# The last block's second product in an AdaLN and mixture-of-adapters kernel: five of seven products on two levels, two seeded in PSUM, and the bias as a row of the adapters' weights

## The chip, the cores and the metric

One core of one Trainium2 chip. The metric is the device time of one execution in microseconds. The kernel before has a median of 261.63 us over 3 runs (261.48 to 261.75).

## What is computed

All in fp32, for 64 batches of 64 tokens with 512 features:

```python
q = relu(cond @ W3 + b3)                          # 64 x 512, one row for each batch
v = relu(((64 * x + x.sum(1)) * q) @ W2 + b2)     # first product, 512 x 512
base = v @ W_base + b_base                        # second product, 512 x 512
gates = softmax(v @ W_router + b_router)          # 6 experts, the two largest are kept
h = v @ [A_s, A_r]                                # 7 adapters of rank 16: 112 columns
out = x + base + (h * [1, kept gates]) @ [B_s; B_r]
```

## The kernel before, in words

The tokens are cut into four blocks (k = 0 to 3), each of two halves h of 512 tokens; features lie on the partitions, in four chunks of 128. A block goes through a first product (W2), the adapters' and router's product `ph` (8 groups of 128 tokens), the gate, and a second product (W_base).

Both products use a scheme of seven block products in place of eight: features in two halves, tokens in two halves, with row sums `s` or `sy` (`row_sums`, L255) and weight sums `t2`, `tb` (`weight_sums`, L130). In blocks 1 to 3 the first product applies the scheme a second time within each of the seven (`first_inner`, L424, "two levels"): an inner product is one matmul of 128 x 128 weights with 256 columns (`q`, L443), and seven of them stand for eight. Their inner row sums come from `prepare_inner` (L299), partly on GpSimd (L333), their inner weight sums from `inner_weight_sums` (L144). An inner step has two PSUM banks: `a` holds products 1 and 2 in its low half, 5 and 3 in its high half; `b` holds 6 in the low half, 7 and 4 in the high half. ScalarE copies the low half of `a` to that of `b` (`seed_y`), and that to `b`'s high half (`seed_z`); VectorE or ScalarE take the results out (`take_...`).

The second product (`second`, L616) has one level in all blocks: `prod(i, j, name)` is two matmuls of 512 columns into a bank, `seed` a ScalarE copy from bank to bank, `with_x` (L634) a VectorE step that adds the bank, the bias column `bb_sb` and the rows of x, and `routed` (L640) the adapters' part. `gate` (L574) runs on VectorE with one exponential on ScalarE; the weighting into `hw` (L683) follows; eight transposes (`pt`, L704) turn it; ScalarE copies it to `hwT` (L706), and GpSimd forms the difference `hwd` (L708). In the last block the last two output rows are cut in 384 and 128 columns (L726), with the last output issued from ScalarE's queue.

The order on every engine is the order in which the program is written (`manual_schedule`). The fillers (`behind`, `fill`, `share`) hand out the preparation of block k + 1 during block k, and are empty in the last block. PSUM has six banks that rotate under one tag (`ps_p`) and a tile of two banks (`ps_h`) that `ph` and `pt` use in turn. Loads of x for the residual (`load_rows`, L606) and outputs go through the SP queue, which issues in order.

The last block's tail, as written before (L740 to L752):

```python
        prod(3, 0, "w", start=False)
        routed("w", 0, KH, hwd[:GR])
        leave(ps["w", 0], KH, 0, u12[0])
        ...
        for p, cols, queue in last:
            part(p, cols, 3, False)
            last_routed(p, cols, hwd)
            leave(p, KH + 1, 0, u12[1], cols, queue)
```

Of the kernel before, what the change touches and what calls it, by code (L numbers as in the profile page):

```python
# [32 lines left out]
HC = GR + E  # L33


@with_exitstack
def adaln_ffn(ctx: ExitStack, tc: tile.TileContext, xa, x0, x1, head, w3, w2, wb, a, bcat, br, outT):
# [25 lines left out]
    def load_x(k):  # L63
        xs[k] = xpool.tile([P, NC, 2, TB], F32, tag="x", name=f"x_{k}")
        for c in CHUNKS:
            nc.sync.dma_start(xs[k][:, c].rearrange("p h t -> p (h t)"), x1[k, c])
# [5 lines left out]
    def loaded(src, shape, name):  # L72
        t = const.tile(shape, F32, tag=name, name=name)
        nc.sync.dma_start(t, src)
        return t
# [9 lines left out]
    NH0 = NQ * B + 3 * NC  # L85
    head_sb = const.tile([P, NH0 + NQ * P], F32, tag="head_sb", name="head_sb")
    cond_sb = head_sb[:, : NQ * B].rearrange("p (c b) -> p c b", c=NQ)
    b3_sb, b2_sb, bb_sb = (head_sb[:, NQ * B + n * NC : NQ * B + (n + 1) * NC] for n in range(3))
# [30 lines left out]
    bcat_sb = loaded(bcat, [GR, D], "bcat_sb")  # L119
    load_x(1)  # L120

# [22 lines left out]
    def inner_weight_sums(w, t, name):  # L144

        at = {i: n for n, i in enumerate((5, 6, 7, 4, 1, 2, 3))}
        it = const.tile([P, 4, 7, P], F32, tag=name, name=name)

        def side(o, n):
            b = {1: t[o][:, 0, :P], 2: t[o][:, 1, :P], 3: t[o][:, 1, P:]}  # L150
            return b[n] if n in b else it[:, {5: 0, 6: 1, 7: 2, 4: 3}[n], at[o]]

        low = w.rearrange("p (o k) m -> p o k m", k=KH)
        groups = ((slice(0, 4), lambda c, m: t["sums"][:, :, c, ts(m, P)]),
                  (slice(4, 6), lambda c, m: low[:, :, c, ts(m, P)]),
                  (slice(6, 7), lambda c, m: t[3][:, c, ts(m, P)].unsqueeze(1)))
        steps = []
        for o, b in groups:
            i = [it[:, n, o] for n in range(4)]
            steps += [  # L160
                lambda i=i, b=b: nc.vector.tensor_tensor(i[0], b(0, 1), b(0, 0), ALU.subtract),
                lambda i=i, b=b: nc.vector.tensor_tensor(i[1], b(1, 1), i[0], ALU.subtract),
                lambda i=i, b=b: nc.vector.tensor_tensor(i[2], b(1, 1), b(0, 1), ALU.subtract),
                lambda i=i, b=b: nc.vector.tensor_tensor(i[3], b(1, 0), i[1], ALU.subtract),
            ]
        return side, steps
# [88 lines left out]
    def row_sums(a, name, cols=slice(0, TB)):  # L255

        all_s = mid.tile([P, 4, KH, TB], F32, tag=name, name=name)
        s = [all_s[:, i, :, cols] for i in range(4)]
        a11, a12, a21, a22 = a[:, :KH, 0, cols], a[:, KH:, 0, cols], a[:, :KH, 1, cols], a[:, KH:, 1, cols]

        def steps(c=slice(0, KH)):
            return [
                lambda: nc.vector.tensor_tensor(s[0][:, c], a21[:, c], a22[:, c], ALU.add),
                lambda: nc.vector.tensor_tensor(s[1][:, c], s[0][:, c], a11[:, c], ALU.subtract),
                lambda: nc.vector.tensor_tensor(s[2][:, c], a11[:, c], a21[:, c], ALU.subtract),
                lambda: nc.vector.tensor_tensor(s[3][:, c], a12[:, c], s[1][:, c], ALU.subtract),
            ]

        return {1: a11, 2: a12, 3: s[3], 4: a22, 5: s[0], 6: s[1], 7: s[2], "sums": all_s}, steps
# [3 lines left out]
    def fill(n):  # L273
        for _ in range(min(n, len(behind))):
            for step in behind.pop(0):
                step()
# [21 lines left out]

    def prepare_inner(k):  # L299
# [13 lines left out]
        def steps(g, a, engine=nc.vector):  # L313
            return [
                lambda: engine.tensor_tensor(s[g][:, 0], a(0, 1), a(1, 1), ALU.add),
                lambda: engine.tensor_tensor(s[g][:, 1], s[g][:, 0], a(0, 0), ALU.subtract),
                lambda: engine.tensor_tensor(s[g][:, 2], a(0, 0), a(0, 1), ALU.subtract),
                lambda: engine.tensor_tensor(s[g][:, 3], a(1, 0), s[g][:, 1], ALU.subtract),
            ]

# [103 lines left out]
    def first_inner(k, y):  # L424
# [94 lines left out]
        for step in inner[k]["late"]:  # L519
            step()  # L520
        fill(2)
# [52 lines left out]
    def gate(k, ph):  # L574
# [10 lines left out]
        nc.scalar.activation(g, lg, AF.Exp)  # L585
        sm = small.tile([P, 2 * NS], F32, tag="sm", name=f"sm_{k}")
# [11 lines left out]
        nc.vector.tensor_tensor(eq, gj, ge, ALU.is_equal)  # L598
        nc.vector.tensor_tensor(gt, gj, ge, ALU.is_gt)
        nc.vector.tensor_tensor(eq, eq, tri.unsqueeze(1).to_broadcast(pair), ALU.mult)  # L600
        nc.vector.tensor_tensor(gt, gt, eq, ALU.add)
        rank = small.tile(shape, F32, tag="rank", name=f"rank_{k}")
# [13 lines left out]
    def second(k, y, ph, res):  # L616
# [17 lines left out]
        def with_x(name, j, f, h):  # L634

            t = row(f, h)
            nc.vector.scalar_tensor_tensor(t, ps[name, j], bb_sb[:, f : f + 1], t, ALU.add, ALU.add)  # L637
            return t
# [9 lines left out]
        def part(p, cols, i, start):  # L648
            for c in range(KH):
                nc.tensor.matmul(  # L650
                    p[:, cols], tb[i][:, c, ts(1, P)], sy[i][:, c, cols], start=start and c == 0, stop=False,
                    skip_group_check=True,
                )

        def last_routed(p, cols, hw):
            nc.tensor.matmul(
                p[:, cols], bcat_sb[:, ts(KH + 1, P)], hw[:GR, cols], start=False, stop=True,
                skip_group_check=True,
            )

        def leave(p, f, h, add, cols=slice(0, TB), queue=nc.sync):
            nc.vector.tensor_tensor(add[:, cols], p[:, cols], add[:, cols], ALU.add)
            queue.dma_start(outT[k, f, h, :, cols], add[:, cols])
# [5 lines left out]
        def share():  # L669
# [12 lines left out]
        hw = small.tile([P, 2 * NS, GR], F32, tag="hw", name=f"hw_{k}")  # L682
        nc.vector.tensor_tensor(  # L683
            hw.rearrange("p s (g r) -> p s g r", r=R),
            ph[:, :, :GR].rearrange("p s (g r) -> p s g r", r=R),
            w.unsqueeze(3).to_broadcast([P, 2 * NS, G, R]),
            ALU.mult,
        )
# [12 lines left out]
        pt = ps_h.tile([P, 2 * NS, P], F32, tag="ph", name=f"pt_{k}")  # L701
        hwT = small.tile([P, 2, TB], F32, tag="hwT", name=f"hwT_{k}")
        for s in range(2 * NS):
            nc.tensor.transpose(pt[:GR, s, :], hw[:, s, :], ident)  # L704
        for h in range(2):
            nc.scalar.copy(hwT[:GR, h], pt[:GR, ts(h, NS)].rearrange("p s t -> p (s t)"))  # L706
        hwd = small.tile([P, TB], F32, tag="hwd", name=f"hwd_{k}")
        nc.gpsimd.tensor_tensor(hwd[:GR], hwT[:GR, 0], hwT[:GR, 1], ALU.subtract)  # L708
# [4 lines left out]
        routed("x", 0, 0, hwT[:GR, 0])  # L713
        finish("x", 0, 0, 0)
        routed("z", 0, 0, hwT[:GR, 1])
        finish("z", 0, 0, 1)

        routed("w", 0, KH, hwT[:GR, 1])
        leave(ps["w", 0], KH, 1, u22[0])
        share()  # L720
        if k < NB - 1:
            prod(5, 1, "w")
            routed("w", 1, KH + 1, hwT[:GR, 1])
            leave(ps["w", 1], KH + 1, 1, u22[1])
        else:
            last = [(ps_p.tile([P, TB], F32, tag="pp", name=f"last_{lo}"), slice(lo, hi), queue)  # L726
                    for lo, hi, queue in ((0, 3 * P, nc.sync), (3 * P, TB, nc.scalar))]
            for p, cols, queue in last:
                part(p, cols, 5, True)
                last_routed(p, cols, hwT[:, 1])  # L730
                leave(p, KH + 1, 1, u22[1], cols, queue)
        share()
        routed("x", 1, 1, hwT[:GR, 0])
# [3 lines left out]
        routed("z", 1, 1, hwT[:GR, 1])  # L737
# [3 lines left out]
        routed("w", 0, KH, hwd[:GR])  # L741
        leave(ps["w", 0], KH, 0, u12[0])
        share()
        if k < NB - 1:
            prod(3, 1, "w", start=False)
            routed("w", 1, KH + 1, hwd[:GR])
            leave(ps["w", 1], KH + 1, 0, u12[1])
            return
        for p, cols, queue in last:
            part(p, cols, 3, False)  # L750
            last_routed(p, cols, hwd)
            leave(p, KH + 1, 0, u12[1], cols, queue)  # L752
# [4 lines left out]
    inner_t, inner_steps = inner_weight_sums(w2_sb, t2, "inner_t")  # L757
    for k in range(NB):
# [14 lines left out]
        if not rest:  # L773
            groups.sort(key=lambda g: g[1] // KH)
        for n, (h, s) in enumerate(groups):
            if rest and n == 2:
                rest()
            for c in range(NC):
                nc.tensor.matmul(  # L779
                    ph[:, h * NS + s, :HC], y[:, c, h, ts(s, P)], a_sb[:, c, :],  # L780
                    start=(c == 0), stop=(c == NC - 1),
                )
        sys_[k], steps = row_sums(y, "sy")
# [54 lines left out]
```

## Time and profile before

| | |
|---|---|
| median of the runs | 261.63 us |
| the profiled execution: time | 261.56 us |
| its span in the trace | 259.8 us |
| last `ph` matmul ends, last block | 224.69 us |
| last matmul ends | 256.56 us |
| TensorE / VectorE / ScalarE / GpSimd busy | 254.8 / 193.9 / 136.5 / 38.7 us |
| copy of a bank of 512 columns on ScalarE (L629) | 571 to 573 ns |
| two-input add on VectorE, 256 / 512 / 1024 columns | 418 / 688 / 1219 ns |
| two-input add on GpSimd, 256 / 512 columns | 727 / 1270 ns |
| one output of 256 KB, issue to landing | 2.0 us |

The span runs from the first to the last event of the trace; the time of the execution has 1.76 us around it. In a row of the timeline the columns are the start, the duration, the engine, the line, the operation with output and inputs, and in brackets how long the engine sat idle before and what it waited for. In the chain the columns are start, duration, and what. PE is TensorE, PEld its weight loads, DVE VectorE, ACT ScalarE, POOL GpSimd, SPq and ACTq the DMA issues of those queues.

### The profile page before, as it was taken

How to read it: one execution, taken by the hardware profiler on the slowest of the kernel's cores; microseconds unless marked ns; L12 is line 12 of the kernel's file. 1: busy time of each engine (PE TensorE's matmuls, PEld its weight loads, DVE VectorE, ACT ScalarE, POOL GpSimd, SP SyncE). 2: the span in 40 equal slices, each digit the busy share in tenths (PEclk: the TensorE clock that was granted, in tenths of full speed). 3: DMA queues.
4: the chain of work that ended last, by engine and by line, in shares of the span. 5: the costliest groups of instructions: out<-in, count | busy, mean ns of one | idle time of the engine just before them, and what ended most of it. 6: DMA issues, size and time to landing. Idle time of an engine off the chain costs nothing.

```text
span 259.8 us, 3177 instructions
## 1 busy us (share of the span) xinstructions
PE 254.8 (98%) x1004; PEld 164.5 (63%) x1004; DVE 193.9 (75%) x386; ACT 136.5 (53%) x373; POOL 38.7 (15%) x53
## 2 busy tenths in 40 slices
PE   7999999999999999999999999999999999999995
PEld 3756896454478888444458889544447889745453
DVE  2899898799968967968995894988895475872332
ACT  2399496596048896289017889349404428112000
POOL 1000000020017610002006630002001770000100
PEclk9999999999999999999999999999999999999999
DMA  6997629303320044000521025200332023400233
GB/s 194 360 352 295 261 99 390 156 3 121 121 81 0 11 156 161 0 3 6 196 81 42 0 83 168 76 0 3 121 121 81 0 77 92 159 0 3 76 139 108
DMA packets 14145, 28.54 MB, mean 110 GB/s; under 512 B 1472, under 2 KB 2496, under 8 KB 14128
## 3 DMA queue, kind: packets, MB, share of 16 engines
q1 hardware_dynamic: 13840, 28.21, 30.6%
q8 instruction: 8, 0.13, 0.2%
q10 hardware_dynamic: 288, 0.13, 0.2%
q14 instruction: 9, 0.07, 0.1%
HBM read 19.94 MB, written 8.39 MB: 109 GB/s over the span
## 4 chain that ended last, share of the span: by engine, by line
PE 94%; ACT 2%; DMA 2%; SPq 0%; issue 0%; DVE 0%
PE ia L446 13%; PE ph L779 11%; PE oz L170 11%; PE ox L170 11%; PE ib L446 10%; PE ow L170 9%; PE py L354 5%; PE oy L170 5%; PE ow L641 5%; PE oz L641 3%; PE ox L641 3%; DMA w_sb<-in_w_dram 2%; PE yw L170 1%; PE pt L704 1%; PE last L650 1%; PE yz L170 1%
## 5 line engine op out<-in xcount | busy, mean ns | idle before, releaser
L212 ACT ACTIVATE x<-x,vsum,nq 128x64 f32<-128x64 f32 x192 | 67.5, 431 | 7.0 <-DVE vsum L208 7.0
L779 PE MATMUL ph<-a_sb,y 128*128 128x118 f32 x256 | 30.5, 276 | 0.3 <-ACT y L340 0.3
L779 PEld LDWEIGHTS ph<-a_sb,y 128*128 128x128 f32 x256 | 30.0, 192 | 1.2 <-ACT y L340 0.7
L437 DVE TENSOR_TENSOR u<-ib,u 128x256 f32<-128x256 f32 x42 | 16.4, 419 | 18.5 <-PE ib L446 18.3
L452 ACT COPY ib<-ia 128x256 f32<-128x256 f32 x21 | 7.6, 361 | 42.3 <-PE ia L446 42.3
L170 PE MATMUL ox<-y,wb_sb 128*128 128x512 f32 x64 | 29.5, 593 | 0.0
L708 POOL TENSOR_TENSOR hwd<-hwT 112x512 f32<-112x512 f32 x4 | 5.8, 1452 | 136.1 <-ACT hwT L706 136.1
L170 PEld LDWEIGHTS ox<-y,wb_sb 128*128 128x128 f32 x64 | 11.9, 190 | 13.4 <-issue 13.2
L437 DVE TENSOR_TENSOR u<-ia,u 128x256 f32<-128x256 f32 (+1 forms) x36 | 16.1, 462 | 2.9 <-ACT u L484 1.6
L446 PE MATMUL ib<-inner_s,inner_t 128*128 128x256 f32 x60 | 17.8, 384 | 0.0
L340 ACT ACTIVATE y<-u,head_sb 128x256 f32<-128x256 f32 (+1 forms) x30 | 15.8, 585 | 3.8 <-DVE u L412 3.2
L637 DVE SCALAR_TENSOR_TENSOR xu<-oz,head_sb,xu 128x512 f32<-128x512 f32 x16 | 12.0, 749 | 7.3 <-PE oz L170 4.8
L207 DVE TENSOR_REDUCE vsum<-x 128x8 f32<-128x512 f32 x24 | 16.2, 676 | 0.0
L170 PE MATMUL oz<-sy,tb 128*128 128x512 f32 x32 | 15.2, 599 | 0.0
L170 PE MATMUL oz<-y,tb 128*128 128x512 f32 x32 | 15.1, 593 | 0.0
L170 PE MATMUL oy<-sy,tb 128*128 128x512 f32 x32 | 15.0, 592 | 0.0
L354 PE MATMUL py<-v,w_sb 128*128 128x512 f32 (+1 forms) x40 | 14.4, 510 | 0.7 <-DMA w_sb<-in_w_dram 0.7
L170 PE MATMUL ow<-sy,tb 128*128 128x512 f32 x28 | 13.2, 592 | 0.0
L170 PE MATMUL ow<-sy,wb_sb 128*128 128x512 f32 x28 | 13.2, 592 | 0.0
L455 ACT COPY ib<-ib 128x256 f32<-128x256 f32 x21 | 7.6, 363 | 10.0 <-PE ib L446 10.0
L446 PEld LDWEIGHTS ib<-inner_s,inner_t 128*128 128x128 f32 x60 | 11.2, 190 | 2.2 <-ACT ib L455 0.8
L250 ACT ACTIVATE v<-x,vsum,nq 128x64 f32<-128x64 f32 x32 | 11.0, 427 | 1.7 <-DVE vsum L248 1.7
(173 smaller groups left out, 461.6 us busy)
## 6 DMA issues: line engine op xcount, KB each, us to landing
xu<-in_x_dram SPq DMA_DIRECT2D x16, 512.0 KB, 4.2
out_dram<-xu SPq DMA_DIRECT2D x30, 256.0 KB, 2.0
x<-in_x_dram SPq DMA_DIRECT2D x12, 512.0 KB, 7.5
x<-in_x_dram SPq DMA_DIRECT2D x7, 256.0 KB, 5.7
w_sb<-in_w_dram SPq DMA_DIRECT2D x4, 256.0 KB, 5.5
wb_sb<-in_wb_dram SPq DMA_DIRECT2D x4, 256.0 KB, 4.9
w_sb<-in_w_dram SPq DMA_DIRECT2D x1, 384.0 KB, 4.7
out_dram<-xu SPq DMA_DIRECT2D x2, 192.0 KB, 1.9
```

The lines of the kernel that those rows point to most:

```text
L170: nc.tensor.matmul(ps, w[i][:, c, ts(j, P)], s[i][:, c, :], start=start and c == 0, stop=c == KH - 1, skip_group_check=True,)
L207: nc.vector.tensor_reduce(vsum[:, c, bs], xc, AX.XY, ALU.add)
L212: nc.scalar.activation(x, x, AF.Identity, bias=vsum[:, c, b : b + 1], scale=nq[:, c, b : b + 1])
L250: nc.scalar.activation(v[:, c, :, ts(b, NH)], batches_of(c, b, b + 1)[:, :, 0], AF.Identity, bias=vsum[:, c, b : b + 1], scale=nq[:, c, b ...
L340: nc.scalar.activation(y[:, f, h, cols], src, AF.Relu, bias=b2_sb[:, f : f + 1])
L354: nc.tensor.matmul(p[:, :, lo * NH : hi * NH], w2_sb[:, c, ts(f, P)], v[:, c, :, lo * NH : hi * NH], start=(c == 0 and lo == 0), stop=(c = ...
L437: add = lambda o, a, b: nc.vector.tensor_tensor(o, a, b, ALU.add)
L446: nc.tensor.matmul(bank[b, t][:, cols], t_side(o, n), s_side(o, n), start=n == 1, stop=True, skip_group_check=True,)
L452: nc.scalar.copy(bank["b", t][:, lo], bank["a", t][:, lo])
L637: nc.vector.scalar_tensor_tensor(t, ps[name, j], bb_sb[:, f : f + 1], t, ALU.add, ALU.add)
L641: nc.tensor.matmul(ps[name, j], bcat_sb[:, ts(f, P)], hw, start=False, stop=True, skip_group_check=True)
L779: nc.tensor.matmul(ph[:, h * NS + s, :HC], y[:, c, h, ts(s, P)], a_sb[:, c, :], start=(c == 0), stop=(c == NC - 1),)
```

## The change

For blocks 0 to 2 `second` stays, with the bias no longer added by `with_x` but carried as row 113 of `bcat_sb`, against a column of ones in `hw`. In the last block `second` is replaced by `second_inner`: products 1, 2, 5, 4 and 3 on two levels (steps t = 0 to 4), products 6 and 7 on one level, each in a bank that ScalarE first fills with the partial sum it is to be added to. Three of its inner products stand between the groups of `ph`. GpSimd forms the inner weight sums in block 2, and in the last block most of the inner row sums, one of the outer ones, and two sums of outputs. The diff, cut to its core:

```diff
-            nc.vector.scalar_tensor_tensor(t, ps[name, j], bb_sb[:, f : f + 1], t, ALU.add, ALU.add)
+            nc.vector.tensor_tensor(t, ps[name, j], t, ALU.add)
...
+    bcat_sb = const.tile([GB, D], F32, tag="bcat_sb", name="bcat_sb")
+    nc.sync.dma_start(bcat_sb[:GR], bcat)
     load_x(1)
+    nc.sync.dma_start(bcat_sb[GR:], bb)
...
+        if k == NB - 2:   # first_inner, after the late sums; steps[4:] follow after hwd
+            wide["t"], wide["steps"] = inner_weight_sums(wb_sb, tb, ..., (5, 4), nc.gpsimd)
+            for step in wide["steps"][:4]:
+                step()
...
+    def gate(k, ph, between=()):   # others() after the exponential, after eq, and ahead of rank
...
+        order = (1, 2, 5, 4, 3)
+        place = {1: (0, (0, 1, 2, 3)), 2: (1, (0, 1, 2, 3)), 5: (1, (3, 1, 2, 0)), 4: (2, (0, 1, 2, 3)),
+                 3: (3, (0, 1, 2, 3))}
+        run(sums_of(1, of_y(0, 0), nc.gpsimd))
+        def row_side():
+            run(sums_of(2, of_y(KH, 0)))
+            got, steps = row_sums(y, "sy")
+            sy.update(got)
+            steps = steps(fourth=nc.gpsimd)
+            run(steps[:3])
+            fourth.extend(steps[3:])
+        def late_sums():
+            run(sums_of(5, of_s(5), nc.gpsimd))
+            run(sums_of(4, of_y(KH, 1), nc.gpsimd))
+            run(fourth)
+            run(sums_of(3, of_s(3), nc.gpsimd))
...
+        def passed_on(t, j, cols):
+            o = order[t]
+            if o == 5:
+                add(x12[:, j, cols], x12[:, j, cols], p5[:, j, cols])
+            if o in (4, 3):
+                ...
+                queue = nc.scalar if o == 3 and cols == hi else nc.sync
+                queue.dma_start(outT[...], out[o][:, j, cols])
...
+        def first_part():     # ahead of the seventh group of ph
+            open_banks(0); q(1, 0); q(5, 0); seed_y(0); take_w5(0)
+        def second_part():    # ahead of the eighth
+            q(6, 0); seed_z(0); take_u(0)
+        def one_level(i, j, name, seed):
+            bank[name, j] = ps_p.tile([P, TB], F32, tag="pp", name=f"o{name}_{k}_{j}")
+            nc.scalar.copy(bank[name, j], seed)
+            product(bank[name, j], i, j, tb, sy, start=False)
+        def main_part(ph):
+            open_banks(1); q(1, 1); q(5, 1); seed_y(1)
+            def on_tensor():
+                q(7, 0); q(3, 0); q(6, 1); seed_z(1); q(2, 0); take(0, bank["a", 0], lo, 0, lo)
+            def evict_first():
+                take_22(0); take_w5(1)
+            gate(k, ph, (on_tensor, evict_first, lambda: add(p1[:, 1, lo], bank["a", 0][:, hi], p1[:, 1, lo])))
+            q(4, 0); take_21(0); q(7, 1); take_22(1); take_u(1); q(3, 1); q(2, 1)
+            weigh(k, ph)
+            late_sums()
+            take_1(1)
+            one_level(6, 0, "y", p1[:, 0])
+            one_level(6, 1, "y", p1[:, 1])
+            q(4, 1)
+            add(x12[:, 0], bank["y", 0], x12[:, 0])
+            take_21(1)
+            add(x12[:, 1], bank["y", 1], x12[:, 1])
+            one_level(7, 0, "z", bank["y", 0])
+            hwT = turn(k)                 # eight transposes, two ScalarE copies
+            one_level(7, 1, "z", bank["y", 1])
+            for j in range(KH):
+                for x in (x21, x22):
+                    add(x[:, j], bank["z", j], x[:, j])
+            add(x11, x11, p1, nc.gpsimd)
+            hws["less"] = difference(k, hwT)[:GB]
+            for t in (2, 3):
+                open_banks(t); q(1, t); q(5, t); seed_y(t); take_w5(t)
+            for j in range(KH):
+                accumulate(pr[:, j], bcat_sb[:, ts(j, P)], hwT[:GB, 0], True)
+            q(2, 2); q(6, 2); take_u(2); seed_z(2); q(3, 2); routed(2, 1); q(6, 3); take_u(3); seed_z(3)
+            q(7, 2); routed(2, 22); take_22(2); q(2, 3); take_1(2)
+            open_banks(4); q(1, 4); q(5, 4); seed_y(4); q(4, 2); routed(2, 4); take_21(2)
+            add(x22, x22, p5, nc.gpsimd)
+            leave(KH, 1, x22)
+            q(7, 3); routed(3, 22); take_22(3); take_w5(4); q(3, 3); q(6, 4); seed_z(4); routed(3, 1)
+            add(x11, pr, x11)
+            leave(0, 0, x11)
+            take_1(3); q(4, 3); routed(3, 4); take_21(3); q(7, 4); routed(4, 22); take_22(4); take_u(4)
+            q(3, 4); q(2, 4); routed(4, 1); take_1(4); q(4, 4); routed(4, 4); take_21(4)
```

Several calls of the new code are written on one line here, and the comments are added. `q(n, t)` is inner product n of step t, `take_...` moves a part of a bank out with an add (VectorE) or a copy (ScalarE), `routed` adds the adapters' part to the step's banks, `leave` issues two outputs on SP.

## The prediction, made before the change was run

> **What bounds the kernel now.** I read the page first (shares, slices, chain), then the chain of waits over the last block, then the queues of ScalarE and VectorE there, then the transfers.
>
> ```profile
> PE 254.8 (98%) x1004; PEld 164.5 (63%) x1004; DVE 193.9 (75%) x386; ACT 136.5 (53%) x373; POOL 38.7 (15%) x53
> PEclk9999999999999999999999999999999999999999
> PE 94%; ACT 2%; DMA 2%; SPq 0%; issue 0%; DVE 0%
> ```
>
> TensorE is busy 98% of 259.8 us at full clock, and it is 94% of the chain. The chain's end, in order of time (start, us, what):
>
> ```profile
> 219.34 5.35 PE ph L779 x48
> 224.69 3.44 PE ox L170 x8
> ...
> 238.43 0.87 PE pt L704 x8
> 239.31 1.72 PE oz L170 x4
> ...
> 256.33 0.24 PE last L656 x2
> 256.56 0.02 issue
> 256.59 0.29 DVE xu L662
> ```
>
> From 224.69 (end of `ph`) to 256.56 TensorE never waits: 31.87 us. After it come 0.29 us of VectorE and 2.92 us until the span ends at 259.8. So the last block pays for every matmul removed, and for every wait put in: its tail hides nothing.
>
> **How matmuls cost.** A matmul of fp32 shows as two instructions. Four of 128x512 take 1.72 us (`oz` above), 0.43 each; the two-level code of the first product gives, in order of start:
>
> ```profile
> 205.73 0.59 PE L446 MATMUL ia<-s,t 128*128 128x256 f32 x2
> 206.16 0.59 PE L446 MATMUL ia<-x,w_sb 128*128 128x256 f32 x2
> 206.60 0.59 PE L446 MATMUL ia<-inner_two,inner_t 128*128 128x256 f32 x2
> ```
>
> One inner product per 0.43 us (start to start; "0.59" includes draining). A product on one level is 4 x 0.86 = 3.44 us = 8 such units; on two levels it is 7 units = 3.01 us.
>
> **How banks are passed on.** ScalarE and VectorE rows of the last block:
>
> ```profile
> 207.28 0.36 ACT L452 COPY ib<-ia 128x256 f32<-128x256 f32 x1 [0.99 <-PE ia L446]
> 235.64 0.75 DVE L637 SCALAR_TENSOR_TENSOR xu<-oy,head_sb,xu 128x512 f32<-128x512 f32 x1 [1.57 <-ACT oz L629]
> 239.34 1.07 ACT L706 COPY hwT<-pt 112x512 f32<-112x512 f32 x2 [3.74 <-PE pt L704]
> ```
>
> The seed copy at 207.28 reads the half that the matmuls of 206.16 wrote, yet starts after those of 206.60 (drained at 207.19), which wrote the other half. At 235.64 VectorE reads a bank that TensorE finished at 235.0, but waits for ScalarE's *read* of it (235.03 to 235.60). And `hwT`'s first copy starts after all eight transposes (239.31), not after four. So two engines never share a bank, and order is the program's.
>
> **What the Trainium skill says.** "PSUM — Partial Sum Buffer", section "PSUM bank collisions raise a hardware error", says that the scheduler adds a dependency between instructions of different engines on one bank, reads too; the three rows agree. The same page, "Engine vs sequencer instructions": ScalarE, VectorE and GpSimd queues are strict FIFO; the trace contradicts it nowhere. "GPSIMD Engine Reference", section 3.1, puts a two-input add at 1.96 times VectorE's time; here 727 against 418 ns at 256 columns, 1.27 against 0.69 us at 512: agrees roughly. "DMA: Bandwidth & Descriptors", "Issuing engines are not separate DMA queues": DMAs of both queues share 16 engines; at 257.25 to 258.25 one transfer of each queue is drained together.
>
> **The change, part by part.**
>
> *Matmuls.* Products 1, 2, 5, 4, 3 at 7 units instead of 8: 5 x 0.43 = **-2.15 us**. Products 6 and 7 stay at 3.44 each. Routed matmuls: before 8 of 0.86; now 2 of 0.86 (`pr`) and 12 of 0.43: equal, 6.9 us. The transposes stay eight. Three units (q1, q5, q6 of product 1) move between `ph`'s groups: `ph` ends at 224.69 + 3 x 0.43 = 225.98.
>
> *Bias as a row.* K is 113 instead of 112, and columns set the time: nothing. VectorE's bias add falls from 0.75 to 0.69 us eight times a block; VectorE waits for TensorE there, so nothing. The DMA of `bb` is one more issue on SP (0.33 us) after `load_x(1)`; what follows it is the load of block 2, not due before 90 us: nothing. `bcat_d` makes GpSimd wait for it, with nothing behind it until the first `hwd` at 56.9.
>
> *Inner sums of the weights.* Four adds of 0.73 us (spaced 0.70) stand in block 2 behind the late sums that end at 144.5, so the `e3` add moves from 146.7 to about 147.4; both halves are done near 149.9, and its reader starts at 151.6: hidden by 1.7 us. The other eight follow `hwd` in block 2 on an idle GpSimd: nothing. If covers fail: below 1 us each.
>
> *Row sums.* On VectorE four adds of 256 columns (1.6 us) in the gap of 1.25 us ahead of 221.04, and the fourth 1.22 us add leaves it: it is free at about 225.0, before `ph` ends. GpSimd: `sums_of(1)` 216.7 to 219.6, due at 223; `sums_of(5)` must wait for q(3,1) (same places), near 230.5, then 2.8 + 2.8 + 2.35 + 2.8 us to 241.3; readers come at 242 or later. Covers, thin for product 5's successor, cost under 1 us if gone. (2.35 for 1024 columns is my estimate from 0.73 at 256 and 1.27 at 512.)
>
> *Waits that are added.* Three, all on TensorE in order.
>
> First, q(4,0) overwrites the bank that `take_22(0)` reads. That add stands in VectorE's queue behind half the gate. The exponential stands on ScalarE behind `seed_y(1)`, which waits for q(5,1) (226.84) and ends at 227.23, so the gate slips 0.43. Gate rows from `lg` to `eq` start 1.70 us apart now; with the slip `take_22(0)` runs 228.5 to 228.93. Restart after a ScalarE copy: block 1's `oz` copy ended at 114.40 and four passes ended at 116.44 instead of 1.72 later, so 0.32. q(4,0) goes at 229.25 instead of 225.98 + 6 x 0.43 = 228.56: **0.7 us** (bounds 0 to 1).
>
> Second, the seed of `z0` copies bank `y0`, but the add into `x12` reads that bank first in the program. VectorE from `lg` at 226.0: gate 4.13 (225.72 to 229.85 now) + 0.43 slip + three adds between (0.39 each) = 231.7; `take_22(1)`, `take_u(1)` 0.8, the weighing 1.02, `take_1(1)` 0.69, the add 0.69: 234.9. Copy 0.57 and restart 0.32: 235.8. TensorE arrives after 19 units and the first wait at 225.98 + 8.17 + 0.7 = 234.85: **1.0 us** (0 to 1.4).
>
> Third, the seed of `z1` is issued on ScalarE *behind* the two `hwT` copies, which wait for all transposes, and TensorE has only `z1`'s product after these. Copies 1.07, seed 0.51 more, restart 0.32: **1.95 us** (1.2, if the first copy goes half way, to 2.1). Below nothing is excluded for all three: a wait can't return time.
>
> Later waits I price at nothing: each seed has at least three units (1.3 us) between its reader and its source, against 0.36 + 0.32, and VectorE has about 8 us of adds in the last 12.
>
> TensorE in sum: -2.15 + 0.7 + 1.0 + 1.95 = **+1.5**, so it ends at 258.06.
>
> *Outputs.* Now 2 MB leave in parts from 244.4 on. Afterwards SP's first output is `x22`, behind a 1024-column GpSimd add that needs the last part of product 5. That part (routed(2,4)) ends 16 units, 6.87 us, before TensorE's end: 251.2. Copy 0.4, add 2.35 with hand-over 0.1: 254.05, and all later outputs on SP queue behind it. From issue to first byte: 244.42 to 245.28, 0.86. Rates:
>
> ```profile
> 253.25:253.50 0.25, 0.25 (x2) 0.15 (x1) 0.00 (x0) 0.00 (x0) 0.00 (x0) 1.00 1.04 393
> ...
> 257.50:257.75 0.25, 0.00 (x0) 0.00 (x0) 0.00 (x0) 0.00 (x0) 0.00 (x0) 1.00 1.02 362
> ```
>
> The last column is GB/s: 393 with 2 KB rows at best, less with rows of 1.5 and 0.5 KB mixed. Half of the 2 MB now has 1 KB rows, which no row shows: 2.1 MB take 5.3 us at 393, 6.0 if I interpolate between the two; I take 5.75. Data end: 254.05 + 0.86 + 5.75 = 260.65; now they end at 258.2, and the span 1.6 later. New span **262.25**. If transfers kept pace, TensorE's end + 0.45 (VectorE) + 3.0 would give 261.5. A profiled execution of 261.56 has a span of 259.80, so 1.76 lies around it: **264.0 us**. The median of before, 261.63, lies 0.07 above that execution; I add nothing for it.
>
> **Rivals.**
> - *The transfers keep pace, or `z0` is not late* (0.22): TensorE sets the end, 261.5 + 1.76 = 263.3; without the second wait 263.0. For: VectorE and TensorE reach `z0` within 0.1 us of each other. Against: 2 MB behind one add.
> - *The waits don't bite: faster* (0.07). Place: the two seeds of product 7 and q(4,0). Without any, routed(2,4) ends at 247.5, and the same 11.1 us of copy, add and transfers give 258.6, **260.4 us**. It is faster by over 0.2% only while the waits sum to less than 0.7 us. For: TensorE's saving is certain. Against: the third alone has 1.2 at least, by FIFO order.
> - *Waits near the lower bounds* (0.07): sum about 1.5 us, span 260.1: 261.9, no change.
> - *Dearer GpSimd and rows* (0.14): 1024-column adds slower than extrapolated, 1 KB rows nearer 270 GB/s: 1 us more, 265.0.
> - That the change doesn't cut matmul time is excluded by the 0.43 spacing.
>
> **Numbers.** The likeliest case has 0.50, 264.0. Range 262.3 to 265.4: it takes in the first and fourth rival, and leaves out the two without a loss and a little above. Within 0.2% (0.52 us, about what a measurement here tells from no change) 0.07; faster 0.07; slower 0.86.
>
> **What will show it.** `ph` ending near 226.0; TensorE waiting for VectorE at q(4,0), for ScalarE ahead of `z0` (1 us) and ahead of `z1` after the transposes (2 us); 29.7 us of TensorE work after 224.69; no output before about 254; the DMA slices full from there to the end. Wrong if ScalarE copies `z1` before the transposes end, if outputs start before 251, or if TensorE shows no gap over 1 us in the last block.

## The result, and the profile after

| | before | after |
|---|---|---|
| median of the runs, us | 261.69 (4 runs) | 265.23 (264.94 to 265.37, 4 runs) |
| ratio, with its 95% interval | | 1.0134 [1.0116, 1.0151] |
| the profiled execution: time / span, us | 261.56 / 259.8 | 264.94 / 263.1 |
| block 0, block 2: first `ph` matmul starts | 33.94, 156.50 | 34.37, 157.49 |
| last block: last `ph` matmul ends | 224.69 | 226.91 |
| last matmul ends | 256.56 | 258.40 |
| from there to the end of the span | 3.24 | 4.70 |

The change costs 3.5 us, 1.3%. The shares of the page and of its chain answer to the first lines of the prediction:

```profile
PE 254.0 (97%) x1034; PEld 171.0 (65%) x1034; DVE 199.4 (76%) x404; ACT 142.8 (54%) x391; POOL 67.1 (25%) x86
...
PE 85%; DVE 9%; ACT 3%; issue 0%; DVEq 0%
```

TensorE was 94% of the chain and is now 85%; VectorE has gone from 0 to 9%, but some 18 us of that stand ahead of 30 us, where the chain now runs through VectorE's sums and no longer through TensorE's first product: a change of path, not 18 us of waiting. GpSimd's busy time has gone from 38.7 to 67.1 us. The chain through the last block (start, duration, what) shows where TensorE now waits; before, it did not wait here at all. `ja` and `jb` are the banks `a` and `b` of the inner steps, `oy` and `oz` the banks of products 6 and 7:

```profile
226.91 0.89 PE ja L828 x4
...
229.09 0.46 DVE eq L645
229.54 0.35 DVE parts L784
229.89 0.04 issue
229.94 1.13 PE jb L828 x4
...
235.42 0.43 PE jb L828 x2
...
235.89 1.98 PE oz L176 x4
237.88 0.89 PE pt L604 x8
238.76 0.02 issue
238.79 1.07 ACT hwT L606 x2
239.86 0.50 ACT oz L917
...
240.40 1.98 PE oz L176 x4
...
257.51 0.88 PE jb L828 x4
258.40 0.02 issue
258.42 0.42 DVE xu L784
```

The three waits of the prediction are all there. `jb` at 229.94 is q(4,0). Six units behind the end of `ph` it would be due at 229.5; it waits for the gate's `eq` and for `take_22(0)` (`parts`) queued behind that, and its row is 1.13 long where two units take 0.87: 0.43 + 0.26 = 0.70 us. The first `oz` (`z0`) takes 1.98 instead of 1.72 and starts 0.04 late: 0.30 us. Between `pt` and the second `oz` (`z1`) stand the two `hwT` copies and the seed on ScalarE: 240.40 - 238.76 = 1.64, plus the 0.26, is 1.90 us. ScalarE's queue has the reason, the seed of `z1` behind the copies:

```profile
238.79 1.07 ACT L606 COPY hwT<-pt 113x512 f32<-113x512 f32 x2 [2.95 <-PE pt L604]
239.75 0.60 ACT L917 COPY oz<-oy 128x512 f32<-128x512 f32 x1
```

And the outputs of this block: first the GpSimd add and the SP queue, then the transfers in 40 slices of 253 to 263 us.

```profile
251.94 2.60 POOL L784 TENSOR_TENSOR xu<-xu,parts 128x1024 f32<-128x1024 f32 x1 [5.78 <-ACT parts L862]
```

```profile
254.57 0.83 SPq L913 DMA_DIRECT2D out_dram<-xu  x2
```

```profile
DMA  0000000002999999999999999999999992000000
...
DMA packets 1696, 2.10 MB, mean 210 GB/s; under 512 B 160, under 2 KB 1184, under 8 KB 1696
```

None of them leaves before 254.57; data flow from about 255.4 to 261.3 without a break, 2.1 MB in 5.9 us (354 GB/s). TensorE is finished at 258.40, in the middle of that.

**Where the 3.3 us of span come from** (differences of the two traces, 263.1 - 259.8 in sum):

| piece | us |
|---|---|
| blocks 0 to 3 up to the end of `ph`, without the three units moved there (1.30) | +0.93 |
| two levels: 28.59 of matmul after `ph` (31.49 less the waits) plus 1.30 of those units, against 31.87 | -1.98 |
| three waits: 0.70 + 0.30 + 1.90 | +2.90 |
| last matmul to end of span: 4.70 against 3.24 | +1.46 |

The first piece was in no part of the prediction. It is made, within 0.06 us, of two stalls of VectorE in blocks whose second product the change leaves as it was but for the bias. The first is beside `bcat_d` in block 0 (timeline of VectorE and GpSimd):

```profile
24.08 1.03 POOL L1029 TENSOR_TENSOR bcat_d<-bcat_sb 113x256 f32<-113x256 f32 x1 [22.33 <-DMA bcat_sb<-in_bb_dram]
24.45 1.22 DVE L271 TENSOR_TENSOR s<-v 128x512 f32<-128x512 f32 x1
```

A row sum of 0.68 us takes 1.22. It ends 0.56 after GpSimd's subtraction (24.08 + 1.03 = 25.11), as if it had begun only then; and block 0's `ph` starts 0.43 later than before. The second is in block 2, at `nq`, a step that scales `q` for the next block; VectorE first, then GpSimd:

```profile
147.95 1.06 DVE L212 TENSOR_SCALAR nq<-q_sb 128x16 f32<-128x16 f32 x1
148.93 0.67 DVE L213 TENSOR_REDUCE vsum<-x 128x8 f32<-128x512 f32 x1
149.63 0.60 DVE L214 TENSOR_TENSOR vsum<-vsum,q_sb 128x8 f32<-128x8 f32 x1
```

```profile
147.03 0.73 POOL L170 TENSOR_TENSOR inner_tb<-tb,inner_tb 128x256 f32<-128x256 f32 x1
147.71 2.49 POOL L557 TENSOR_TENSOR inner_late<-u,u 128x512 f32<-128x512 f32 x2
```

The same two engines in the kernel before:

```profile
147.59 0.43 DVE L206 TENSOR_SCALAR nq<-q_sb 128x16 f32<-128x16 f32 x1
```

```profile
146.72 2.49 POOL L543 TENSOR_TENSOR inner_late<-u,u 128x512 f32<-128x512 f32 x2 [2.21 <-DVE u L437]
```

`nq` has 16 columns; in block 0 it takes 0.16 us, here 1.06. It ends when the first of GpSimd's two adds ends (half of 2.49 behind 147.71 is 148.96). Before, that pair started at 146.72 and `nq` ended at 148.02: 1.30 behind it, as now. The second add holds another step in the same way: `vsum<-vsum,q_sb` takes 0.17 us in block 0 and 0.60 here, and ends (150.23) with that add (150.20); before it took 0.59. So the pair had a price in the kernel before as well, which no run here takes away. What is new are the four adds ahead of it. The four inner weight sums push the pair back by 0.99, of which 0.36 is what block 2 is late already (`nq` starts at 147.95, before at 147.59); VectorE, which reads nothing of the pair, is pushed along by the other 0.63, and block 2's `ph` comes 0.56 later still than block 0's.

### The profile page after: what moved, and what is told of

Its sections match the earlier page's. It is cut to its first block, busy times and chain, and to the rows that moved or that the text cites. A ratio compares the mean times of both kernels' runs of the same rounds, so it can differ in the third digit from the quotient of the medians.

```text
span 263.1 us, 3316 instructions
## 1 busy us (share of the span) xinstructions
PE 254.0 (97%) x1034; PEld 171.0 (65%) x1034; DVE 199.4 (76%) x404; ACT 142.8 (54%) x391; POOL 67.1 (25%) x86
## 4 chain that ended last, share of the span: by engine, by line
PE 85%; DVE 9%; ACT 3%; issue 0%; DVEq 0%
PE ia L453 12%; PE ph L1064 11%; PE oz L176 9%; PE ib L453 9%; PE ox L176 8%; PE ow L176 8%; PE oy L176 5%; PE ja L828 4%; PE ow L690 4%; PE jb L828 3%; PE oz L690 2%; PE ox L690 2%; PE idle L187 2%; DVE vsum L234 1%; PE pt L604 1%; ACT y L347 1%
## 5 line engine op out<-in xcount | busy, mean ns | idle before, releaser
L611 POOL TENSOR_TENSOR hwd<-hwT 113x512 f32<-113x512 f32 x4 | 5.6, 1393 | 86.2 <-ACT hwT L606 86.2
L176 PE MATMUL ox<-y,wb_sb 128*128 128x512 f32 x48 | 22.1, 593 | 0.0
L176 PEld LDWEIGHTS ox<-y,wb_sb 128*128 128x128 f32 x48 | 8.9, 190 | 10.0 <-issue 9.8
L307 POOL TENSOR_TENSOR inner_two<-x 128x256 f32<-128x256 f32 x3 | 2.2, 728 | 49.4 <-PE ib L453 49.4
L176 PEld LDWEIGHTS oz<-sy,tb 128*128 128x128 f32 x32 | 5.7, 189 | 9.5 <-issue 5.7
L361 PEld LDWEIGHTS py<-v,w_sb 128*128 128x128 f32 x40 | 7.4, 190 | 6.1 <-issue 4.8
L176 PE MATMUL oz<-y,tb 128*128 128x512 f32 x24 | 11.3, 592 | 0.0
```

Of the source, the lines that this page charges most:

```text
L176: nc.tensor.matmul(ps, w[i][:, c, ts(j, P)], s[i][:, c, :], start=start and c == 0, stop=c == KH - 1, skip_group_check=True,)
L361: nc.tensor.matmul(p[:, :, lo * NH : hi * NH], w2_sb[:, c, ts(f, P)], v[:, c, :, lo * NH : hi * NH], start=(c == 0 and lo == 0), stop=(c = ...
```

## The experiments

My theory after the traces had three independent parts. A: GpSimd steps that read SBUF hold up VectorE's, worth 0.4 to 0.5 us for `bcat_d` and 0.6 for the inner weight sums. B: the seed of `z1` stands behind the `hwT` copies, 1.9 us. C: all outputs start behind one add, so transfers, not TensorE, set the end, worth about 1.1 us. The rivals: to A, that loads or the bias row move the early blocks, or that any busy GpSimd does; to B, that the two-level products are slower than counted or wait for GpSimd's sums, so that the wait only moves to a later product; to C, that TensorE sets the end anyway and the outputs merely follow. Each kernel is the changed one with the edit shown, but for the first. The kernel before ran at 261.71 and 261.69 us beside them.

### The bias row alone, in the kernel before

Edit: the kernel before with `bcat_sb` and `hw` one row or column larger, `with_x` without the bias and the bias's DMA in its place behind `load_x(1)`; no `bcat_d`, no inner sums, the second product unchanged.

> The kernel before with the bias as row 113 of the adapters' weights alone: hw with a column of ones, no bias column in the VectorE steps, no bcat_d, no inner sums, the last block as before. Theory A (costs nothing): within 0.2% of before, 261.7. Rival (the extra DMA of one row, or K of 113, costs something in each block): 0.5 us or more over before.

Measured: 261.34 us, ratio 0.999 [0.9974, 1.0006]. The row costs nothing, neither in the last block nor by its load: block 0's `ph` starts at 33.81, which is 13.32 us behind the first `inner_t` step of VectorE (20.49); in the kernel before it is 13.33, in the changed one 13.86. One rival to A is out.

### `bcat_d` late, and then all inner weight sums late as well

If A holds, the subtraction of `bcat_d` is what lengthened VectorE's row sum in block 0. It moves into `second`, block 2, ahead of the weight sums there:

```diff
-    nc.gpsimd.tensor_tensor(bcat_d, bcat_pairs[:, :, 0], bcat_pairs[:, :, 1], ALU.subtract)
...
+            nc.gpsimd.tensor_tensor(bcat_d, bcat_pairs[:, :, 0], bcat_pairs[:, :, 1], ALU.subtract)
```

> The changed kernel, with the one GpSimd subtraction that forms bcat_d moved from the start (24.1 us) to block 2 behind hwd; the DMA of the bias row stays where it was. Theory A (the subtraction [...] lengthened it from 0.68 to 1.22 us on the path of block 0): block 0's ph begins at 33.94 again instead of 34.37, the time falls by 0.4 us to about 264.8. Rival (the later start of block 0 is from the added DMA, or chance): no change, 265.2.

The second kernel has this too, and moves the first four sums behind `hwd`:

```diff
-            for step in wide["steps"][:4]:
-                step()
...
-            for step in wide["steps"][4:]:
+            for step in wide["steps"]:
```

> As the run with bcat_d late, and all twelve GpSimd steps of the inner weight sums behind hwd in block 2, none among the first product's additions. Theory A: the VectorE step nq at 147.95 takes 0.2 to 0.4 us instead of 1.06, block 2's gap on TensorE near 151 goes, the last block's ph ends 0.9 us earlier than in the changed kernel (226.0), time about 264.3. Rival (the last block alone accounts for the loss): 265.2.

Measured: 264.5 us, 1.0098 [1.0074, 1.0123], and 264.35 us, 1.0089 [1.0062, 1.0116]. The traces are sharper than these, because one stretch belongs to each step:

| stretch, us | before | after | `bcat_d` late | both late |
|---|---|---|---|---|
| first `inner_t` step (VectorE) to block 0's `ph` | 13.33 | 13.86 | 13.33 | 13.32 |
| block 0's `ph` to block 2's `ph` | 122.56 | 123.12 | 123.13 | 122.48 |

Each edit shortens its own stretch, by 0.53 and 0.65 us, and leaves the other alone. The second ends 0.08 below the kernel before, at the 122.48 that the bias row alone also shows. In the kernel with both late `nq` takes 0.43 us, as before the change. A holds as to place and size, 1.2 us in the traces. The medians give 0.73 and 0.88; that the second edit shows as 0.15 there and not as 0.65 is within the intervals of the two, and the profiled execution of the second kernel began 0.74 us late, its first `inner_t` step at 21.25 against 20.51 (the first loads of x land up to 0.8 us apart from one execution to the next).

### Any busy GpSimd, or one that reads SBUF?

`bcat_d` late as above, and in its old place a GpSimd step of about the same length, also held by a DMA of the bias, that reads nothing. It fills a tile that nothing uses. If A holds, the row sum keeps its time, because the step reads nothing in SBUF:

```diff
+    fill_sb = const.tile([P, 896], F32, tag="fill_sb", name="fill_sb")
+    nc.sync.dma_start(fill_sb[:1, :D], bb)
+    nc.gpsimd.memset(fill_sb, 1.0)
```

> As the run with bcat_d late, but with a GpSimd memset of 128 x 896 in its old place, held back by a DMA of the bias row into the same tile, so that it runs near 24 us for about 0.8 us beside VectorE's row sums. It reads no SBUF. Theory A [...]: the row sums stay at 0.68 us each, and from the first inner weight sum on VectorE to ph it takes 13.3 us as in the kernel before. Rival (any GpSimd work, or the arrival of that DMA, disturbs VectorE): one row sum takes 1.1 to 1.2 us and the stretch 13.7 to 13.9.

Measured: 264.34 us in one run, the level of `bcat_d` late. The timeline:

```profile
24.20 0.84 POOL L1032 MEMSET fill_sb<- 128x896 f32 x1 [22.45 <-DMA fill_sb<-in_bb_dram]
24.43 0.68 DVE L271 TENSOR_TENSOR s<-v 128x512 f32<-128x512 f32 x1
```

GpSimd is busy at the same moment and the row sum takes its 0.68 us; the stretch is 13.32. So neither the wait for that DMA nor a busy GpSimd is the cause. What is left is what the two steps do not share: the subtraction reads SBUF, the memset only writes it. The Trainium skill, page "SBUF — State Buffer", section "SBUF: two separate sides", describes this: VectorE and GpSimd share a pair of ports, which is an exclusive lock for a whole instruction; a VectorE step takes part in it in a two-port mode, or, where the GpSimd step reads SBUF, with two SBUF inputs. The trace agrees for the row sum (1.22 beside `bcat_d`, 0.68 beside the memset) and for `vsum<-vsum,q_sb` (0.60 beside a GpSimd add), both with two SBUF inputs; the reduction between the adds, with one, kept its 0.67. For `nq`, with one SBUF input, only the two-port clause could apply; which mode it ran in no trace shows, so for `nq` the mechanism stays open, though not the place and the size.

### The seed of `z1` ahead of the transposes

```diff
+            seeded(1, "z", bank["y", 1])      # the bank and its ScalarE copy
             hwT = turn(k)
...
-            one_level(7, 1, "z", bank["y", 1])
+            product(bank["z", 1], 7, 1, tb, sy, start=False)
```

> The changed kernel, with the ScalarE copy that seeds z1 written ahead of the transposes and of the two hwT copies. Theory A (waits of product 7's seeds move both TensorE and the outputs): TensorE's gap of 1.9 us after the transposes goes, the GpSimd add of x22 and the outputs come 1.9 us earlier, time 263.3. Rival B (the two-level products are themselves slower than counted, or what follows waits for GpSimd's sums instead): the gap moves to a later product, time 264.5 or more.

Measured: 262.87 us, 1.0046 [1.003, 1.0062], 2.36 less than the changed kernel's median. The chain has lost the wait:

```profile
236.14 1.98 PE oz L176 x4
238.12 0.87 PE pt L604 x8
239.00 1.72 PE oz L176 x4
...
255.84 0.88 PE jb L828 x4
```

From the end of `ph` (227.16) to the last matmul it is 29.57 us instead of 31.49: 1.92 less, the wait of 1.90. So no later product took the wait over: B holds, and its rival falls. The outputs come earlier by the same amount, because the last part of product 5, which they wait for, moves with TensorE: counted from the end of `ph` the GpSimd add starts after 250.27 - 227.16 = 23.11 us, against 251.94 - 226.91 = 25.03. The medians differ by 0.44 us more than the traces; that is within the intervals of the two.

### An output ahead

The add of `pr` into `x11` and its two outputs stand right behind `pr`'s matmuls instead of near the end:

```diff
             accumulate(pr ...)
+            add(x11, pr, x11)
+            leave(0, 0, x11)
...
-            add(x11, pr, x11)
-            leave(0, 0, x11)
```

> The changed kernel, with the add of pr into x11 and its two outputs moved to directly behind the pr matmuls (about 7 us earlier), so that 512 KB leave before x22. Theory A (the end is set by draining 2 MB behind the add of x22): the drain ends near 260.1 instead of 261.3, time 264.0 to 264.2. Rival C (TensorE's last matmul and the last output's own latency set the end): no change, 265.2.

Measured: 264.05 us, 1.0085 [1.0062, 1.0107], 1.18 less than the changed kernel. SP's queue:

```profile
247.69 8.18 SPq L913 DMA_DIRECT2D out_dram<-xu  x4
```

A quarter of the 2 MB leaves while nothing else does. TensorE gains nothing (its last matmul ends at 258.89, in an execution whose `ph` of block 0 starts 0.5 later), yet the span ends 3.41 us after that matmul instead of 4.70. C holds: TensorE did not set the end. 1.29 us were the transfers'.

### The three together, and the remaining seeds

The edits of both late, of the seed of `z1` and of the output ahead, in one kernel:

> The changed kernel with the three repairs together: bcat_d and all inner weight sums late, z1's seed ahead of the transposes, x11 out early. Theory A (the losses add: 0.45 + 0.6 + 1.9 + what is left of the drain): the last matmul near 255.5, span near 259.2, time 261.0, 0.2 to 0.3% below before. Rival (a new wait takes their place, such as the GpSimd sums for steps 3 and 4): 262 or more.

The last kernel has these edits, and each seed of product 7 stands directly behind the matmuls that it copies, ahead of the add that reads the same bank; `seed_y(1)` stands behind the gate's exponential:

```diff
             one_level(6, 1, "y", p1[:, 1])
+            seeded(0, "z", bank["y", 0])
             q(4, 1)
             add(x12[:, 0], bank["y", 0], x12[:, 0])
             take_21(1)
+            seeded(1, "z", bank["y", 1])
             add(x12[:, 1], bank["y", 1], x12[:, 1])
...
-            open_banks(1); q(1, 1); q(5, 1); seed_y(1)
+            open_banks(1); q(1, 1); q(5, 1)
             def on_tensor():
+                seed_y(1)
```

> As the run with the three repairs, and each seed of product 7 copied directly behind its source (ahead of the additions of that bank into x12), and the second step's seed_y written behind the gate's exponential. Theory A: TensorE's waits ahead of z0 (0.3 us) and of q(4,0) (0.7 us) shrink to about 0.3 together, time 260.3, 0.5% below before. Rival (VectorE's adds now come later and hold the banks that follow): no better than 261.0.

Measured: 260.89 us, 0.9974 [0.9961, 0.9987], and 260.22 us, 0.9933 [0.9911, 0.9956]. The three parts are nearly independent: alone they gave 0.88, 2.36 and 1.18, together 4.34 of the 4.42. The last kernel's chain in the last block:

```profile
226.19 0.87 PE ja L827 x4
...
228.79 1.13 PE jb L827 x4
...
234.71 1.72 PE oz L176 x4
236.42 0.87 PE pt L602 x8
237.30 1.72 PE oz L176 x4
...
254.15 0.88 PE jb L827 x4
```

All that is left of the waits is 0.26 at q(4,0); TensorE needs 28.84 us after `ph`, against 31.49 in the changed kernel and 31.87 in the kernel before, of which 1.30 stand ahead of `ph`'s end here. So with nearly all its waits gone the change is worth 31.87 - 28.84 - 1.30 = 1.73 us of TensorE, and as it was written that lay buried under them. This version is 0.7% faster than the kernel before, the fastest of all.

## Why the prediction was right, and where its steps failed

The forecast of 264.0 us was 1.2 low, inside its range. Its mechanism, waits worth more than the matmuls saved and transfers at the end, is what happened. By its steps:

| step | predicted | measured |
|---|---|---|
| end of `ph`, last block | 225.98 | 226.91 |
| two levels | -2.15 | -1.98 |
| q(4,0) waits | 0.7 | 0.70 |
| seed of `z0` | 1.0 | 0.30 |
| seed of `z1` | 1.95 | 1.90 |
| last matmul ends | 258.06 | 258.40 |
| first output on SP | 254.05 | 254.57 |
| issue to first data / 2 MB / to the end of the span | 0.86 / 5.75 / 1.6 | 0.85 / 5.9 / 1.8 |
| span | 262.25 | 263.1 |

**What failed: the inner sums of the weights and `bcat_d`, priced at nothing.** The prediction said of the four adds "hidden by 1.7 us" and of `bcat_d` that it waits "with nothing behind it". Both sentences are true of GpSimd's queue and of the tile's readers. They leave out that a GpSimd step beside VectorE's own steps has a price there, 0.53 us in block 0 and 0.65 in block 2 by the two kernels above. The view that would have told was in the profile of before: `nq` at 147.59 took 0.43 us beside a GpSimd add, and ended with it. "If covers fail: below 1 us each" did bound the size, but no cover failed; it was the wrong kind of price.

**The seed of `z0` was over-estimated by 0.7.** VectorE's rows were added end to end from the gate on, giving 8.92 us from the end of `ph` to the add into `x12`; it took 8.33, since rows overlap in the trace (each starts before the shown end of the one before). `z0` being nearly in time was half of a rival; the other half, transfers that keep pace, was false, as the output moved ahead showed. **The two matmul terms** are near: behind the last wait 37 units take 16.01 us, 0.433 each instead of 0.430. What makes up that difference no run shows; the granted clock of this stretch is 1.00.

**The outputs** were right in kind: first output, drain and end all within 0.6 us. The add of 1024 columns took 2.60 us; two others took 2.35 and 2.36, which was the estimate. Of the rival with dearer GpSimd and rows, 265.0, the number came close to the result and the mechanism only in part: 0.25 of the add and some 0.35 of the drain were real, and the rate was 354 GB/s, not 270.

**The sum.** The span is 0.86 longer than forecast: +0.93 in the early blocks, -0.75 of waits, +0.17 of matmuls, and +0.51 after the last matmul. What is left of the 1.2 us is the median of the runs, 0.29 above the profiled execution, and 0.08 because the time around the span is 1.84 us, not 1.76. That the miss is so small is in part luck: the early blocks, priced at nothing, and the seed of `z0`, priced too high, nearly cancel. The bias row cost nothing, as forecast.

## What to carry to other kernels

A step that is put on an idle engine is not free because its queue is empty: look at what VectorE does in the same microsecond, and move GpSimd steps with SBUF inputs to stretches where VectorE does not set the pace. On a full TensorE the saved matmuls paid here only once each seed copy was issued directly behind the matmuls that it copies, ahead of other readers of that bank and of copies that wait for later matmuls. And with 2 MB to write behind one add, the first output should leave as soon as its data exist: here a quarter of the data sent early gave back 1.2 us.

## What the runs showed of the hardware that was not expected

- A VectorE step of 16 columns, 0.16 us alone, took 1.06 us beside GpSimd adds, and a row sum of 0.68 took 1.10 to 1.22 beside `bcat_d`. GpSimd's step was lengthened as well: 1.03 to 1.17 us for 256 columns where 0.73 is usual. A memset of 0.84 us did no harm.
- Not every pair of steps blocks: GpSimd's adds from 231.6 to 239.7 kept 0.72 to 0.74 and 2.35 us beside VectorE's adds with a PSUM input, which kept 0.42 and 0.68 us.
- 2 MB, half of the data in rows of 1 KB, went out at 354 GB/s, against 393 at best with 2 KB rows before.
- The first loads of x land up to 0.8 us apart from one execution to the next, which moves the whole trace; stretches between two marks are steadier (from the first `inner_t` step to block 0's `ph` 13.32 to 13.33 us in all seven kernels without `bcat_d` there).
